# Dealing the maxima of an attention kernel as one stream over all groups, with a lead of three steps

## The chip, the cores and the metric

The kernel runs on one core of one Trainium2 chip. A core has five engines that work beside each other: TensorE (PE in the profile; its weight loads are listed as PEld), VectorE (DVE), ScalarE (ACT), GpSimd (POOL) and SyncE (SP), which here issues DMA transfers. Each engine works through its own queue in the order of the program and waits on semaphores for the others. The metric is the device time of one execution in microseconds (us); less is better.

## The reference

The input x is 4 x 2048 x 256. It is layer-normalised, and the result goes through causal attention with 16 heads of 16 channels with rotary positions, and through a feed-forward network with ternary weights; the output is x plus the attention times the silu of the network.

```python
xn = _layernorm(x)
q, k, v = rope(xn @ Wq.T + bq), rope(xn @ Wk.T + bk), xn @ Wv.T + bv
att = softmax(where(tril, q @ k.T / sqrt(16), -inf))
s = (att @ v) @ Wo.T + bo
g = silu(gelu(xn @ ternary(W1).T + b1) @ ternary(W2).T + b2)
return x + s * g
```

## The kernel before

**Blocks and groups.** The 8192 rows are cut into 16 blocks of 512 rows, four blocks (n = 0, 1, 2, 3) for each batch entry. A block of kind n attends to its own 512 keys and to the n blocks of keys before it, so blocks of kind 0 have the least work and blocks of kind 3 the most. The 16 heads are cut into four groups of four, so the program walks over 64 groups (block, g) in order; below, "group (4,1)" is head group 1 of block 4. Blocks 0, 4, 8 and 12 are of kind 0.

**Two passes for each group.** The softmax takes its maxima first. `maxima(blk, g)` is a Python generator. Each of its steps puts two TensorE products q x k (512 columns each) into two PSUM banks (`s1` in the code, `psum<-kst,qst` in the profile) and has VectorE reduce each of the two to maxima (`mx<-psum`). A group has 8n + 5 steps: 5, 13, 21 or 29. After the last step VectorE reduces the partial maxima (`m<-mx`) and writes them twice into a padded tile (`m_pad<-m`, `m_pad<-m,m_pad`). When the generator is then run to its end, TensorE turns this tile with eight small products (`psum<-id_half,m_pad`, into two banks taken by `two_banks("pt")`) and ScalarE copies the turned maxima to `mT`. I call these eight products the turn. `values(blk, g)` is the second pass. It goes over 4n + 3 units. In a unit TensorE forms scores k x q (`psum<-qst,kst`), adds the turned maxima (`psum<-mT,sel`), ScalarE takes the exponential (`e<-psum`), and TensorE multiplies the exponentials of the unit before by v (`psum<-e,vg`). GpSimd masks the diagonal units. The last products of a group are issued by `end()` after the first unit of the next group; it also copies the sums (`av_sb`) and issues eight small stores of them on SP (`y<-av_sb`, `w<-av_sb`).

**Banks.** PSUM has eight banks. One holds the sums of `values`; the other seven are handed out by `bank` and `two_banks`, which choose by an account (`Course`) that the program keeps while it is written: a cost for each instruction (`work`, line 124, for VectorE, ScalarE and GpSimd) and the time at which each bank should come free. The account chooses banks and nothing else.

**The order around the change.** The main loop (line 1307) runs the units of group i and deals out, between them, the maxima of group i + 1. Each unit has two slots; a slot has a weight, `past` sums the weights passed and `whole` is the sum to be reached. `Paced.to(share)` runs the generator until that share of its work is done. With `whole = sum(slots[:-2]) - END` and END = -100, all steps of group i + 1, with the write to `m_pad`, are out before the last unit's scores. At the end of the group, behind its last unit, `maxs.rest()` (line 1359) issues the turn. So all of the maxima of group i + 1, and no others, lie in group i. Groups of kind 0 have three units. Before the scores of their second unit (u = 1) four steps of the next group are out.

**Loads.** `Loads.go()` is called at the start of each group (line 1311) and when a buffer comes free; it issues on SP the loads of q (`qst<-qd`, 512 KB), of k in chunks (`kst<-kd`, 512 KB each) and of v (`vg<-vd`) up to two groups ahead for q and k. There are three buffers for q, so the q of group i + 2 takes the buffer of group i - 1, which comes free when the last scores of that group have been formed. Since `Loads` goes by head order, the k of group i + 2 follows its q. The same SP queue holds the stores of `av_sb`, the reloads of x (`x_res`), and the reciprocal sums (`rd<-w`, `rw<-rd`).

**Other work in a group.** A projection of a later block (`project`) and a feed-forward pass (`feed`, called gate) are dealt into certain groups; a group with a gate runs it ahead of its units. `further()` pops one step of the output part of the block before (`finish`) at fixed places. In groups (4,2), (8,2) and (12,2) these are `divided` (`yT`) and `projected` (`psum<-yT,woT`), and group g = 3 of these blocks begins with a gate.

Of the kernel before, what the change touches and what calls it, by code (L numbers as in the profile page):

```python
# [37 lines left out]
class Course:  # L38
# [27 lines left out]
    def ready(self, engine, out, ins):  # L66
        t = 0.0
        for ap in ins:
            for k in self.keys(ap):
                if self.by.get(k) != engine:  # L70
                    t = max(t, self.written.get(k, 0.0))
        for k in self.keys(out):
            if self.by.get(k) != engine:
                t = max(t, self.written.get(k, 0.0))
            for other, done in self.read.get(k, {}).items():
                if other != engine:
                    t = max(t, done)
        return t
# [45 lines left out]
    def work(self, engine, op, args):  # L124
        aps = [a for a in args if isinstance(a, bass.AP)]
        out, ins = aps[0], aps[1:]
        n = max(a.free_size() for a in aps)
        if engine == "ACT":
            cost, tail = n / 1.2 + (68 if n > NB else 150), 150
        elif engine == "DVE":  # L130
            cost, tail = n / 0.96 + 67, 135
            if op == "memset":
                cost = n / 0.96 + 60
        else:
            two = op == "tensor_tensor" or op == "scalar_tensor_tensor"
            wide = any(st == 0 and k > 1 for a in ins for st, k in a.ap[1:])
            cost, tail = n * (1.85 if wide else 2.1 if two else 0.9) + 190, 60
        start = max(self.at[engine], self.ready(engine, out, ins))
        self.at[engine] = start + cost
        self.note(engine, out, ins, start + cost + tail)  # L140
# [57 lines left out]
def attention_gated_by_ffn(  # L198
# [38 lines left out]
    FC = FF // P  # L237
    NQ = T // NB
# [205 lines left out]
    def rotation(i, n):  # L444


        wide = pp.tile([P, 2, NB], F32, tag="e", name="wide")[:, 0, :]
        copy = nc.vector.tensor_copy if n == 0 else nc.scalar.copy
        copy(
            wide.rearrange("p (t h f) -> p t h f", t=TT, f=HF),  # L450
            csn[:, i, n * TT : (n + 1) * TT, :].unsqueeze(2).to_broadcast([P, TT, H, HF]),
        )
        yield
        pt = bank("pt")
        for t in range(TT):
            nc.tensor.transpose(
                pt[:, t * P : (t + 1) * P], wide[:, t * P : (t + 1) * P], ident
            )
        if n == 0:
            turn = table0[:, i, :]  # L460
        else:
            turn = pp.tile([P, 2, NB], F32, tag="e", name="turn")[:, 0, :]
        nc.scalar.copy(turn, pt)
        release("pt")
        nc.scalar.dma_start(out=cs[n][i], in_=turn)
# [94 lines left out]
    kst, qst, vst, mTs = {}, {}, {}, {}  # L560
# [12 lines left out]
    def load(blk):  # L573
        xs[blk] = xp.tile([P, TT, D], F32, tag="x", name="xn")
        nc.sync.dma_start(out=xs[blk], in_=x_blk[blk])
# [220 lines left out]
    class Loads:  # L796


        def __init__(self):
            self.free = {"q": 3, "k": 8, "v": 5}  # L800
            self.next = {
                "q": iter(groups),
                "k": iter([(*x, c) for x in groups for c in range(x[0] % NQ + 1)]),
                "v": iter([(*x, c) for x in groups for c in range(x[0] % NQ + 1)]),
            }
            self.head = {k: next(i) for k, i in self.next.items()}
            self.ahead = {"q": 2, "k": 2, "v": 1}
            self.now = 0
# [46 lines left out]
    groups = [(blk, g) for blk in range(NBLK) for g in range(G)]  # L855
    loads = Loads()

    def max_steps(n):


        pairs = range(GH // 2)
        steps = [(c, ((t, j),)) for c in range(n) for t in range(TT) for j in pairs]
        steps += [(n, ((TT - 1, j),)) for j in pairs]
        steps += [(n, ((TT - 2, j), (0, j))) for j in pairs]
        return steps + [(n, tuple((1, j) for j in pairs))]

    def columns(n, c, parts):
        return sum(NB if c < n else (t + 1) * P for t, _ in parts)
# [97 lines left out]
    def value_units(n):  # L966


        pairs, d = range(GH // 2), n * TT
        units = [[((kb, j),) for j in pairs] for kb in range(d + 1)]  # L970
        units.append([((d + 1, j), (d + 3, j)) for j in pairs])
        units.append([tuple((d + 2, j) for j in pairs)])
        return units
# [263 lines left out]
    class Paced:  # L1237
# [6 lines left out]
        def to(self, share):  # L1244
            while self.work and self.done < min(share, 1.0) * self.all - 1e-9:
                next(self.gen, None)
                self.done += self.work.pop(0)
# [3 lines left out]
                pass  # L1251

    K5, PJ, R0 = 6, 8, 19
    CHUNK, BESIDE, SH, END = 200, 300, 0.5, -100
    N_R = 1 + 2 * 2 * (NQ - 1) + 2 * (1 + 12)
    N_Q = TT - 1 + 4 + KC + 4 + TT + 1
    N_T = 2 * 2 * (3 + 2) + N_W - 4
    idle = Paced(iter(()), ())

    def max_work(blk):  # L1260

        n = blk % NQ
        return [columns(n, c, parts) + 80 for c, parts in max_steps(n)]

# [15 lines left out]
    with tc.manual_schedule():  # L1282
        load(0)
        setup()
        rest = Paced(prepare(), [1] * N_R)
        for k, _ in enumerate(project(0)):
            if k == 5 + TT - 1:
                for i in range(2):
                    for _ in rotation(i, 0):
                        pass  # L1290
                rest.to(K5 / N_R)
                gate = feed(0)
                next(gate)
        rest.to(R0 / N_R)
        maxs = Paced(maxima(*groups[0]), max_work(0))
        for k, _ in enumerate(gate):

            rest.to(min(19 + 2 * k + (k > 1), 27 + (k - 4)) / N_R)
            maxs.to((k - 2) / (FC - 2))
            if k == 4:  # L1300
                proj = Paced(project(1), [1] * N_Q)
            if k >= 4:
                proj.to(PJ / N_Q * (k - 3) / (FC - 3))
        maxs.rest()
        rest.rest()
        p0, p1 = 0, 2
        for i, (blk, g) in enumerate(groups):
            n = blk % NQ
            units = len(value_units(n))
            loads.now = i  # L1310
            loads.go()
            nxt = groups[i + 1] if i + 1 < len(groups) else None
            maxs = Paced(maxima(*nxt), max_work(nxt[0])) if nxt else idle
            projs, hids = beside(blk)
            if g in projs:
                proj.rest()
                b2, over = projs[g]
                proj = idle
                if b2 < NBLK:
                    proj, p0, p1 = Paced(project(b2), [1] * (N_Q + N_T)), g, g + over  # L1320

            fast = hids.get(g, NBLK) < NBLK
            slots = [CHUNK] * FC if fast else []
            for u in range(units):
                w = NB if u < units - 1 else NB // 2
                w += 80 + (BESIDE if proj is not idle else 0)
                slots += [w * SH, w * (1 - SH)]
            whole = sum(slots[:-2]) - END
            past = 0
            if fast:  # L1330
                for k, _ in enumerate(gate):
                    past += slots.pop(0) if k < FC else 0

                    if k % 3 == 2:
                        maxs.to(past / whole)
            steps = values(blk, g)
            for u in range(units):
                past += slots.pop(0)
                maxs.to(past / whole)
                next(steps)  # L1340
                if u == units - 2:
                    further()
                past += slots.pop(0)
                maxs.to(past / whole)
                next(steps)
                if u == 0 and ends:
                    ends.pop(0)()
                if u == units // 2 and hids.get(g + 1, NBLK) < NBLK:
                    if b2 == hids[g + 1]:
                        proj.rest()  # L1350
                    gate = feed(hids[g + 1])
                    next(gate)
                if proj is not idle:
                    proj.to(1.05 * (g + (u + 1) / units - p0) / (p1 - p0))
                further()
            for _ in steps:
                pass
            loads.release("q")
            maxs.rest()
            if g == G - 1:  # L1360
                proj.rest()
        for do in ends:
            do()
        for do in deferred:
            if do:
                do()
# [55 lines left out]
```

## Time and profile before

| what | value |
|---|---|
| median of 3 runs (lowest, highest) | 2332.27 us (2331.68, 2336.6) |
| the profiled execution's own time | 2329.72 us |
| its span | 2328.0 us |
| TensorE busy | 2188.2 us (94%), weight loads 1213.3 us (52%) |
| VectorE busy | 1606.3 us (69%) |
| ScalarE busy | 1459.8 us (63%) |
| GpSimd busy | 876.2 us (38%) |
| reductions `mx<-psum` | 2176, mean 683 ns |
| mean granted TensorE clock | 0.985 |

The profiled execution took 2.55 us less than the median of the runs, and its span is 1.72 us shorter than its own time. In the profile's rows "<-" between engines means "waited for". A row of the waits gives the sum of us, the number of waits and the longest. A row of the timeline gives start, length, engine, operation, tiles and in brackets the idle time ahead of it with what ended it. All instructions carry the line of one helper (L161), so rows are told apart by their tiles.

### The profile page before, as it was taken

What the parts mean: (1) busy time and instruction counts of PE and PEld (TensorE: products, weight loads), DVE (VectorE), ACT (ScalarE), POOL (GpSimd) and SP (SyncE); (2) the same over time, 40 slices, a digit from 0 to 9 for tenths busy, and PEclk for the clock granted to TensorE, in tenths of its full rate; (3) what the DMA queues carried; (4) which work ended last, traced back from release to release, by engine and by line L of the source; (5) the groups of instructions that cost most, each with busy time, mean ns of one, the idle gap of its engine ahead of it and who ended that gap; (6) DMA issues with size and microseconds to landing.
All of it is one profiled execution on the core that took longest, in us unless ns stands there. A gap on an engine that the chain in (4) does not pass through costs nothing.

```text
span 2328.0 us, 42716 instructions
## 1 busy us (share of the span) xinstructions
PE 2188.2 (94%) x16596; PEld 1213.3 (52%) x16596; DVE 1606.3 (69%) x2782; ACT 1459.8 (63%) x1697; POOL 876.2 (38%) x1198
## 2 busy tenths in 40 slices
PE   5889999999999999999999999999999999999997
PEld 4555545545455555545545464555555555455553
DVE  8667677776556677687635768768763666777881
ACT  4555656656766565765766565666677556666675
POOL 2137252144534525315344543422534462521000
PEclk8899999999999999999999999999999999999998
DMA  7345344243344525234134443513514353442311
GB/s 228 105 149 172 103 158 128 56 137 108 98 149 128 198 69 166 79 105 156 48 121 142 156 144 102 173 55 102 170 42 158 125 173 101 151 129 55 98 48 34
DMA packets 247611, 280.32 MB, mean 120 GB/s; under 512 B 108784, under 2 KB 143728, under 8 KB 247408
## 3 DMA queue, kind: packets, MB, share of 16 engines
q1 hardware_dynamic: 243680, 271.95, 37.1%
q10 hardware_dynamic: 3728, 5.64, 0.7%
q8 instruction: 131, 2.15, 0.4%
q14 instruction: 72, 0.59, 0.1%
HBM read 181.08 MB, written 87.52 MB: 115 GB/s over the span
## 4 chain that ended last, share of the span: by engine, by line
PE 77%; DVE 12%; ACT 5%; POOL 2%; issue 2%; DMA 1%; ACTq 0%; SPq 0%; DVEq 0%; POOLq 0%
PE psum L161 77%; DVE mx L161 7%; ACT e L161 2%; DVE m_pad L161 1%; ACT L161 1%; DMA kst<-kd 1%; DVE tern L161 1%; POOL xn L161 1%; ACT hh L161 1%; ACT h L161 1%; DVE st L161 0%; POOL xl L161 0%; DVE m L161 0%; POOL xh L161 0%; DVE s L161 0%
## 5 line engine op out<-in xcount | busy, mean ns | idle before, releaser
L161 DVE TENSOR_REDUCE mx<-psum 128x1 f32<-128x512 f32 (+2 forms) x2176 | 1362.2, 683 | 520.0 <-PE psum L161 507.6
L161 ACT ACTIVATE e<-psum 128x1024 f32<-128x1024 f32 x1088 | 1062.5, 1022 | 556.0 <-PE psum L161 547.0
L161 PE MATMUL psum<-kst,qst 64*128 64x512 f32 (+3 forms) x2560 | 561.3, 423 | 36.7 <-ACT e L161 13.6
L161 PE MATMUL psum<-e,vg 128*32 128x512 f32 (+3 forms) x5120 | 577.4, 541 | 0.5 <-POOL e L161 0.5
L161 POOL TENSOR_SCALAR_AFFINE_SELECT e<-e 128x256 f32<-128x256 f32 (+1 forms) x448 | 193.8, 448 | 932.2 <-ACT e L161 924.7
L161 PEld LDWEIGHTS psum<-kst,qst 64*128 64x128 f32 x2560 | 295.0, 186 | 428.6 <-DVE mx L161 243.5
L161 PE MATMUL psum<-qst,kst 64*128 64x512 f32 (+3 forms) x2560 | 478.4, 390 | 20.0 <-DVE mx L161 15.8
L161 PE MATMUL psum<-mT,sel 64*128 64x512 f32 (+3 forms) x2560 | 447.5, 365 | 0.4 <-ACT mT L161 0.4
L161 PEld LDWEIGHTS psum<-qst,kst 64*128 64x128 f32 x2560 | 234.4, 187 | 166.0 <-ACT e L161 65.4
L161 PEld LDWEIGHTS psum<-mT,sel 64*128 64x128 f32 x2560 | 233.8, 187 | 27.8 <-ACT mT L161 1.5
L161 POOL TENSOR_TENSOR hl<-h,hh 128x512 fp32r<-128x512 f32 x128 | 165.2, 1299 | 146.7 <-ACT h L161 114.6
L161 PEld LDWEIGHTS psum<-e,vg 128*32 128x32 f32 x5120 | 112.1, 109 | 135.8 <-issue 115.8
L161 POOL TENSOR_TENSOR r<-qk,cos_sin 128x512 f32<-128x512 f32 x56 | 72.7, 1302 | 192.3 <-DMA cos_sin<-cs 117.8
L161 ACT ACTIVATE hh<-psum,b1c 128x512 fp32r<-128x512 f32 x128 | 88.3, 690 | 87.5 <-PE psum L161 87.2
L161 PE MATMUL psum<-xf,wqkvT 128*128 128x512 f32 x256 | 121.0, 608 | 0.9 <-ACT xf L161 0.9
L161 PE MATMUL psum<-xh,w1T 128*128 128x512 f32 x256 | 105.1, 411 | 3.2 <-DVE s L161 2.7
L161 PE MATMUL psum<-hh,w2T 128*128 128x512 f32 x256 | 107.2, 419 | 0.2 <-ACT w2T L161 0.2
L161 PE MATMUL psum<-xl,w1T 128*128 128x512 f32 x256 | 103.1, 403 | 1.5 <-POOL xl L161 1.5
L161 PE MATMUL psum<-hl,w2T 128*128 128x512 f32 x256 | 102.5, 400 | 0.2
L161 PE MATMUL psum<-mask_k,mask_q 64*128 64x128 bf16 (+1 forms) x1280 | 99.3, 213 | 0.0
L161 ACT ACTIVATE qk<-psum,bqk 128x512 f32<-128x512 f32 x64 | 44.1, 689 | 85.8 <-PE psum L161 85.8
L161 ACT ACTIVATE h<-psum,b1c 128x512 f32<-128x512 f32 x128 | 87.8, 686 | 0.0
(125 smaller groups left out, 1551.5 us busy)
## 6 DMA issues: line engine op xcount, KB each, us to landing
kst<-kd SPq DMA_DIRECT2D x160, 512.0 KB
qst<-qd SPq DMA_DIRECT2D x64, 512.0 KB
vg<-vd SPq DMA_DIRECT2D x160, 166.0 KB
qd<-qkhi SPq DMA_DIRECT2D x32, 512.0 KB
qd<-qklo SPq DMA_DIRECT2D x32, 512.0 KB
kd<-qkhi SPq DMA_DIRECT2D x30, 512.0 KB
kd<-qklo SPq DMA_DIRECT2D x30, 512.0 KB
vd<-v SPq DMA_DIRECT2D x16, 574.0 KB
```

Of the source, the lines that this page charges most:

```text
L161: made = call(*args, **kwargs)
```

## The change

The maxima are dealt out by one object, `Ahead`, that lives over all groups. It counts steps, not columns. In group i it is led to `ends[i + 1] + LEAD` with LEAD = 3, `ends` being the running sum of the groups' steps; so when group i ends, the maxima of group i + 1 are all out and three steps of group i + 2 as well. A step is taken only if the program has already issued the loads of the q and k chunk that it reads (`ready`). `whole` is now the sum of all slots, the last unit's too. The turn of group i + 1 is issued by `turn` ahead of the scores of group i's last unit, and not behind them. In a group of kind 0 the counts after its six slots become 1, 2, 3, 4, 5 and 5 (of 5): the first two are the last two steps of group i + 1, and the third, ahead of the scores of unit u = 1, is the first step of group i + 2. In the account, a VectorE step costs at least 205 ns.

```diff
-            cost, tail = n / 0.96 + 67, 135
+            cost, tail = max(n / 0.96 + 67, 205), 135
...
-    CHUNK, BESIDE, SH, END = 200, 300, 0.5, -100
+    CHUNK, BESIDE, SH, LEAD = 200, 300, 0.5, 3
...
+    class Ahead:
+        def __init__(self):
+            self.i, self.done, self.left, self.gen = -1, 0, 0, None
+            self.ends, self.turns = [], {}
+            for blk, _ in groups:
+                self.ends.append((self.ends or [0])[-1] + len(max_steps(blk % NQ)))
+        def ready(self):
+            if self.left:
+                blk, g = groups[self.i]
+                c = max_steps(blk % NQ)[-self.left][0]
+            elif self.i + 1 < len(groups):
+                (blk, g), c = groups[self.i + 1], 0
+            else:
+                return False
+            return (blk, g) in qst and (blk, g, c) in kst
+        def to(self, count):
+            while self.done < count - 1e-9 and self.ready():
+                if not self.left:
+                    self.i += 1
+                    self.left = len(max_steps(groups[self.i][0] % NQ))
+                    self.gen = maxima(*groups[self.i])
+                next(self.gen)
+                self.left -= 1
+                self.done += 1
+                if not self.left:
+                    self.turns[self.i] = self.gen
+        def turn(self, i):
+            if i < len(groups):
+                for _ in self.turns.pop(i):
+                    pass
...
-        maxs = Paced(maxima(*groups[0]), max_work(0))
+        maxs = Ahead()
...
-            maxs.to((k - 2) / (FC - 2))
+            maxs.to(min((k - 2) / (FC - 2), 1) * maxs.ends[0])
...
-        maxs.rest()
+        maxs.to(maxs.ends[0])
+        maxs.turn(0)
...
-            nxt = groups[i + 1] if i + 1 < len(groups) else None
-            maxs = Paced(maxima(*nxt), max_work(nxt[0])) if nxt else idle
+            due = maxs.ends[min(i + 1, len(groups) - 1)] + LEAD
+            begun = maxs.done
...
-            whole = sum(slots[:-2]) - END
+            whole = sum(slots)
...
             for u in range(units):
                 past += slots.pop(0)
-                maxs.to(past / whole)
+                maxs.to(begun + past / whole * (due - begun))
+                if len(slots) == 1:
+                    maxs.turn(i + 1)
                 next(steps)
...
             loads.release("q")
-            maxs.rest()
```

More of the change, by code (lines that the diff above doesn't have):

```diff
@@ L1258, in attention_gated_by_ffn @@
     idle = Paced(iter(()), ())
-    def max_work(blk):
-        n = blk % NQ
-        return [columns(n, c, parts) + 80 for c, parts in max_steps(n)]
+    class Ahead:
[28 more added lines that the diff above has]
+                    pass
     def beside(blk):
@@ L1338, in attention_gated_by_ffn @@
                 past += slots.pop(0)
-                maxs.to(past / whole)
+                maxs.to(begun + past / whole * (due - begun))
+                if len(slots) == 1:
+                    maxs.turn(i + 1)
                 next(steps)
@@ L1343, in attention_gated_by_ffn @@
                 past += slots.pop(0)
-                maxs.to(past / whole)
+                maxs.to(begun + past / whole * (due - begun))
+                if len(slots) == 1:
+                    maxs.turn(i + 1)
                 next(steps)
```

## The prediction

> **What bounds the kernel now.** I read the page first: the engines' shares and the chain that ended last.
>
> ```profile
> PE 2188.2 (94%) x16596; PEld 1213.3 (52%) x16596; DVE 1606.3 (69%) x2782; ACT 1459.8 (63%) x1697; POOL 876.2 (38%) x1198
> PE 77%; DVE 12%; ACT 5%; POOL 2%; issue 2%; DMA 1%; ACTq 0%; SPq 0%; DVEq 0%; POOLq 0%
> ```
>
> TensorE is busy for 2188.2 of 2328.0 us, so all of its idle time is 139.8 us, the start and the tail included. A change in the order of VectorE's work can only win from that. The second view is the waits of TensorE (sum, number, longest).
>
> ```profile
> PE psum L161 <- DVE m_pad L161: 34.8, 46, 1.6
> PE psum L161 <- DVE mx L161: 22.8, 51, 3.8
> PEld psum L161 <- ACT mT L161: 14.6, 38, 0.7
> PE psum L161 <- DMA kst<-kd: 2.5, 3, 1.1
> ```
>
> The largest wait is that of the turn for `m_pad`: 46 of the 64 group ends, 0.76 us each. The timeline of one such end, group (6,3) to (7,0), shows its shape, VectorE first and then TensorE:
>
> ```profile
> 1013.09 1.29 DVE L161 TENSOR_REDUCE mx<-psum 128x2 f32<-128x512 f32 x2 [0.20 <-PE psum L161]
> 1014.41 0.25 DVE L161 TENSOR_REDUCE m<-mx 128x16 f32<-128x96 f32 x1
> 1014.70 0.28 DVE L161 CAST m_pad<-m 128x16 fp32r<-128x16 f32 x1
> 1015.01 0.18 DVE L161 TENSOR_TENSOR m_pad<-m,m_pad 128x16 fp32r<-128x16 f32 x1
> ```
>
> ```profile
> 1014.32 0.40 PE L161 MATMUL psum<-mT,sel 64*128 64x256 f32 x4
> 1015.33 0.43 PE L161 MATMUL psum<-id_half,m_pad 64*68 64x64 f32 x8 [0.62 <-DVE m_pad L161]
> ```
>
> The last reductions, m and the two writes take 2.1 us on VectorE (1013.09 to 1015.19); TensorE has only the last unit's scores and one product with v to lay over them, and then stands still. Afterwards VectorE is empty and waits for the first step of the next group.
>
> The third view is the short groups of kind 0, where loads are late already. SP and TensorE, group (4,1), which starts at 670.89:
>
> ```profile
> 672.34 0.43 SPq L161 DMA_DIRECT2D x_res<-in_L_attn_x_dram  x1
> 672.82 0.50 SPq L161 DMA_DIRECT2D vg<-vd  x1
> 673.42 0.44 SPq L161 DMA_DIRECT2D qst<-qd  x1
> 673.91 0.47 SPq L161 DMA_DIRECT2D kst<-kd  x1
> ```
>
> ```profile
> 675.66 0.50 PE L161 MATMUL psum<-kst,qst 64*128 64x384 f32 x4
> 681.61 0.50 PE L161 MATMUL psum<-kst,qst 64*128 64x512 f32 x2 [0.97 <-DMA kst<-kd]
> ```
>
> The k for group (4,3) is issued at 673.91 and lets TensorE go at 681.61, 7.7 us later. It is used just after group (4,1) has ended, and even so TensorE waits 0.97 us. The row at 675.66 is the step ahead of the scores of unit u = 1.
>
> **Part 1: the turn's wait goes.** In a group of 29 steps the last one for group i + 1 is dealt at 26/29 = 0.90 of the slots, and three further steps lie between it and the turn: six reductions, 6 x 0.683 = 4.1 us of VectorE work behind `m_pad`. When TensorE issues the turn, most of these have been fed, so `m_pad` is done. The wait is removed whole: 34.8 us less the part in blocks of kind 0, which I count in part 3 (waits by window: 1.4 us in each of blocks 4, 8 and 12 and 1.5 us in block 0, in all 5.7): 29.1 us.
>
> What is late next? Behind the turn, TensorE waits again for a bank (0.26 us on `mx` at 1017.43, the same 0.26 at 2232.68), since VectorE begins from nothing. If all 46 ends had it, that is 12 us, and if the steady stream has it too, 0. I take 5. Against it, the turn takes two banks and ScalarE's copy to `mT` (580 ns) in the midst of a unit, while up to three steps hold six of the seven banks. The nearest row is the wait of weight loads for `mT`, 14.6 us over 38 times, which is there already and merely moves; at worst it doubles and all of it shows. So the part is worth between 29.1 - 14.6 = 14.5 and 29.1 + 12 = 41 us; I take 29.1 + 5 = 34. VectorE's total is unchanged: the number of steps is the same, and only their places differ.
>
> **Part 2: the floor in the account.** It touches no instruction, only which bank is chosen. The steps concerned (`m` 203 to 253 ns, `m_pad` 328 and 293 ns, `bn_aggr` 182 ns) come nearer to their measured lengths. Bank waits of TensorE (22.8 on `mx`, 13.6 on `e`) bound what choices can do, in either direction; few choices lie just behind these steps. I take 0, with 5 us to each side.
>
> **Part 3: the lead meets loads that are not there.** In groups of 13 to 29 steps the first step of group i + 2 comes at 0.77 of the group or later, over 10 us after the loads were issued (the shortest is group (5,2): issued at 792.8, due at 788.3 + 0.77 x 20.0 = 803.7): hidden. A group of kind 0 has five steps, and the step ahead of the scores of u = 1 reads q and k of group i + 2, issued at the start of the same group; `ready` does not stop it, since in program order the load has been issued. TensorE stands there, and behind it on its queue the scores of u = 1, hence ScalarE's exponentials and everything after.
>
> Landing: from the first issue at 672.34 to 681.61, x_res, v, q and k (512 + 166 + 512 + 512 = 1702 KB) take 9.27 us, 184 KB/us. I use that rate for the others.
> - (4,0): v store, v, q and k (574 + 166 + 512 + 512 KB) from 659.53: k of (4,2) lands at about 669.1. The step was at 666.35; with one step fewer ahead of it (0.5) and a bank wait gone (0.2), TensorE arrives at 665.7 and waits 3.4 us. The turn's 0.69 and the 0.2 are saved: the group ends 2.5 us late.
> - (4,1): arrives at 675.66 + 2.5 - 0.9 = 677.3. The loads on SP stand behind the `av_sb` stores, issued ahead of the first stall, so they come no later; k lands at about 681. Wait 3.7. With 0.69 and 0.97 saved the group's successor starts 3.5 us late.
> - (4,2): its loads follow `rw<-rd` at 683.76 (256 + 166 + 512 + 512 KB, 7.9 us: 691.7), some 1.4 us later by the delay of `av_sb`: 693.1. TensorE arrives at 686.13 + 3.5 - 0.9 = 688.7 and waits 4.4. Behind it lie 8.4 us of work up to the gate of (4,3) (686.13 to 694.64, less 0.15 of a wait for `yT`). It starts at 701.5 and not at 694.64: 6.8 us lost.
>
> The gate of (4,3) is fed by GpSimd's splits, which come after the exponential and mask of u = 1, so they are delayed alike. Block 8 is like block 4 (6.8). In block 12 no store of v stands ahead: q and k from 1786.98 land 5.6 us later, about when TensorE arrives; with the first wait gone I take 5. In block 0 the k of (1,0) is issued at 127.12, behind four stores of k; by the two rates of landing (5.6 us for q and k from 125.82, or 7.7 from 127.12) it is there at 131.4 to 134.8, say 132.5. The step was at 125.96; the 5.7 us from it to the gate at 131.66 hold 1.5 us of wait for `m_pad`. The gate starts at 132.5 + 4.2 = 136.7: 5 us lost. In all 2 x 6.8 + 5 + 5 = 23.6 us, between 14 (each landing 2 us sooner) and 32 (each 2 us later).
>
> [...]
>
> **The sum.** 34 saved, 23.6 lost: 10 us less. The profiled execution's own 2329.72 becomes 2320; against the median of the runs, 2332.27, it is 2322.
>
> **The rivals.**
> - No new wait for loads (chance 0.22): the k lands earlier because less is queued ahead of it than the rate says; part 1 stands alone, 34 less: 2298. For it speaks that the first such load (661.91) is read at 671.13 with no wait; against it the 7.7 us row.
> - Slower by the loads (0.20): in the three groups of a kind-0 block the waits add up in full (3.4 + 3.7 + 4.4 = 11.5, three blocks, and 5 in block 0: 40) because what I count as saved (bank waits, the turn's waits) is spent on other waits. The point is 34 / 4 = 8.5 us for each block: above it the change loses. 40 - 34 = 6 more: 2338.
> - The turn's wait only changes its name (0.16): the turn in the midst of a unit waits for two banks, at half of the 14.6, with no refill gain: 29.1 - 7.3 - 23.6 = 2 more: 2334.
>
> **How the numbers follow.** My forecast, waits gone at the long groups and loads late at the short ones, has 0.42. What a measurement of this kernel can tell from no change is about 0.2%, 4.7 us. Faster: 0.36 of the forecast's 0.42, all 0.22 of the first rival and 0.02 of the third: 0.60. Same: 0.06 + 0.03 (second) + 0.08 (third): 0.17. Slower: 0.17 + 0.06: 0.23. The range runs from 2298, the first rival's middle (11 in 100 below it), to 2341, the second rival's 2338 with 3 us of the unknown landing: 19 in 100 are left out. The forecast's own range is 2307 to 2332.
>
> **What would show it.** Right: the wait of `psum` for `m_pad` nearly gone; a wait for `kst<-kd` of some 35 to 45 us in about ten places, all in the first three groups of blocks 4, 8 and 12 and in (0,2); long groups 0.6 to 0.9 us shorter. Wrong: no kst wait above 5 us in all (first rival), waits for `mx` or `e` ahead of the turn or the last scores of 10 us or more (third), or blocks 4, 8 and 12 over 8.5 us longer in their first three groups (second).

## The result and the profile after

The changed kernel takes 2340.8 us (median of 18 runs, 2336.05 to 2342.48) against 2331.8 us before (18 runs): a ratio of 1.0035 with a 95% interval of 1.0026 to 1.0043. It is slower, by little but clear of the noise, and stands at the top of my stated range (2298 to 2341). The profiled execution has a span of 2339.3 us, 11.3 more than before.

The page of the changed kernel first, engines and chain:

```profile
PE 2188.5 (94%) x16596; PEld 1219.1 (52%) x16596; DVE 1606.2 (69%) x2782; ACT 1457.9 (62%) x1697; POOL 875.4 (37%) x1198
PE 76%; DVE 8%; ACT 7%; DMA 4%; issue 3%; POOL 2%; SPq 1%; ACTq 0%; POOLq 0%; DVEq 0%
```

TensorE's busy time is the same to 0.3 us, so all 11 us are idle time. In the chain VectorE has gone from 12% to 8%, and DMA from 1% to 4%. The waits of TensorE, changed kernel, say the same (sum, number, longest):

```profile
PE psum L161 <- DMA kst<-kd: 39.3, 10, 8.7
PE psum L161 <- ACT e L161: 21.7, 40, 0.9
PE psum L161 <- DVE mx L161: 16.2, 39, 0.9
...
PE psum L161 <- POOL e L161: 6.4, 5, 1.5
```

The row for `m_pad`, 34.8 us before, is gone; that for `kst<-kd` has grown from 2.5 to 39.3 us, and `e` (13.6 before) and the mask of GpSimd (0.5) took back 14 us.

The end of group (6,3) in the changed kernel, VectorE and then TensorE:

```profile
1016.20 0.25 DVE L161 TENSOR_REDUCE m<-mx 128x16 f32<-128x96 f32 x1
1016.48 0.18 DVE L161 CAST m_pad<-m 128x16 fp32r<-128x16 f32 x1
1016.69 0.18 DVE L161 TENSOR_TENSOR m_pad<-m,m_pad 128x16 fp32r<-128x16 f32 x1
1016.79 2.47 DVE L161 TENSOR_REDUCE mx<-psum 128x1 f32<-128x512 f32 x4
```

```profile
1018.95 0.50 PE L161 MATMUL psum<-kst,qst 64*128 64x512 f32 x2
1019.28 0.38 PE L161 MATMUL psum<-id_half,m_pad 64*68 64x64 f32 x8
1019.49 0.48 PE L161 MATMUL psum<-qst,kst 64*128 64x256 f32 x4
```

`m_pad` is written 2.4 us before the turn reads it, VectorE goes straight on, and none of these rows has a bracket. That is the gain. The loss is in the short groups. The chain of waits of the changed kernel between 661 and 704 us, groups (4,0) to (4,2) (start, length, what; with pieces left out):

```profile
660.81 6.10 DMA kst<-kd
...
671.77 6.09 DMA kst<-kd
...
685.19 7.03 DMA kst<-kd
...
694.84 1.83 POOL e L161 x4
...
700.10 1.27 POOL xl L161
...
701.40 0.76 DVE s L161
...
702.20 2.09 PE psum L161 x3
```

Three loads of k stand in the chain for 19.2 of 43 us, one behind the other. From the third the chain runs over the exponential, GpSimd's mask, its splits for the gate, VectorE's `s`, and only then TensorE.

To see where the time lies I compare the starts of the copies of `av_sb`, one for each group, in both traces. From the copy of the last group before block 4 to that of group (4,3): 65.3 us before, 75.6 after, so 10.3 lost; block 8 10.4, block 12 14.4, block 0 6.0: 41.2 us lost in the blocks of kind 0. The groups of kinds 1, 2 and 3 (the "long groups" below) have gained 9.2, 7.9 and 11.5: 28.6 us. The rest, 1.3 us, is gained at the start and in the tail. 41.2 - 28.6 - 1.3 are the 11.3 us of the span.

### The profile page after: what moved, and what is told of

The parts are those of the page before. It is cut to its first block, busy times and chain, and to the rows that moved or that the text cites. A ratio compares the mean times of both kernels' runs of the same rounds, so it can differ in the third digit from the quotient of the medians.

```text
span 2339.3 us, 42621 instructions
## 1 busy us (share of the span) xinstructions
PE 2188.5 (94%) x16596; PEld 1219.1 (52%) x16596; DVE 1606.2 (69%) x2782; ACT 1457.9 (62%) x1697; POOL 875.4 (37%) x1198
## 4 chain that ended last, share of the span: by engine, by line
PE 76%; DVE 8%; ACT 7%; DMA 4%; issue 3%; POOL 2%; SPq 1%; ACTq 0%; POOLq 0%; DVEq 0%
PE psum L161 76%; DVE mx L161 5%; ACT e L161 3%; DMA kst<-kd 2%; ACT L161 1%; ACT hh L161 1%; SPq L161 1%; ACT h L161 1%; ACT g L161 1%; POOL e L161 1%; DVE m_pad L161 0%; ACT mT L161 0%; POOL xl L161 0%; DMA vg<-vd 0%; DMA rd<-w 0%
## 5 line engine op out<-in xcount | busy, mean ns | idle before, releaser
L161 PE MATMUL psum<-kst,qst 64*128 64x512 f32 (+3 forms) x2560 | 575.4, 425 | 71.9 <-DMA kst<-kd 39.3
L161 PE MATMUL psum<-qst,kst 64*128 64x512 f32 (+3 forms) x2560 | 491.9, 389 | 19.6 <-DVE mx L161 9.9
L161 PE MATMUL psum<-mT,sel 64*128 64x512 f32 (+3 forms) x2560 | 459.2, 368 | 0.0
L161 PEld LDWEIGHTS psum<-qst,kst 64*128 64x128 f32 x2560 | 246.6, 189 | 116.7 <-ACT e L161 51.8
L161 PEld LDWEIGHTS psum<-mT,sel 64*128 64x128 f32 x2560 | 242.1, 189 | 25.3 <-ACT mT L161 0.2
L161 ACT CAST mT<-psum 68x512 fp32r<-68x512 f32 x64 | 37.2, 581 | 99.1 <-PE psum L161 99.1
```

What stands on the lines that cost most here:

```text
L161: made = call(*args, **kwargs)
```

## The experiments

Each is given as its difference from the changed kernel, unless it says from before; ratios are to the kernel before, run on the same chip. "Short groups" below is the sum over the blocks of kind 0, against before, by the same copies of `av_sb`; like every sum of waits it is read from one profiled execution of each run.

**1. No lead in the short groups.**

```diff
-            due = maxs.ends[min(i + 1, len(groups) - 1)] + LEAD
+            lead = 0 if n == 0 and g < G - 1 else LEAD
+            due = maxs.ends[min(i + 1, len(groups) - 1)] + lead
...
-                if len(slots) == 1:
+                if len(slots) == 1 and lead:
...
+            if not lead:
+                maxs.turn(i + 1)
```

> The changed kernel, but in the first three groups of the blocks of kind 0 (0, 4, 8, 12) the lead is 0 and the turn stands behind the last unit as before; everywhere else lead 3 and the early turn. Theory (the loss is loads asked for too early in the short groups, the gain of the long groups is real): the waits of TensorE for kst fall from 39.3 us to under 4 us, the wait for m_pad stays under 8 us, and the time is about 28 us under the kernel before: 2300 to 2308. Rival 1 (the early turn, which takes two banks in the midst of a unit, or the steady stream costs in the long groups): no faster than before, 2328 to 2345. Rival 2 (the account's floor has re-dealt the banks for the worse): 2315 to 2335, since only a part is removed.

Measured: 0.997 (0.9958 to 0.9982), 2325.75 us. Faster than before, but not by 28 us: the wait for `kst` is down to 2.2 us, yet TensorE waits 15.3 us for `m_pad` in 7 places; without lead and with the new pace a short group's last step comes only in its last unit. Short groups: 18.9 us lost. My number was wrong by 18 us, in the main for a part I had left in, which experiment 5 takes out. The time lies in the range of rival 2 (the floor), which this run does not exclude; experiments 3 and 6 do.

**2. The turn behind the last unit, lead 3.**

```diff
-                if len(slots) == 1:
-                    maxs.turn(i + 1)
...
             loads.release("q")
+            maxs.turn(i + 1)
```

> The changed kernel with lead 3 everywhere, but the turn stands behind the last unit as before. Theory: the same as the changed kernel within 6 us (2335 to 2346), since the lead alone has m_pad ready and the loads are as late as before; the wait for kst stays at 35 to 43 us. Rival 1 (the early turn costs): 10 us or more faster than the changed kernel, under 2331.

Measured: 1.0053 (1.0038 to 1.0069), 2344.27 us, within the theory's range and not separable from the changed kernel. The place of the turn trades: the long groups gain 19.4 us in place of 28.6, the short ones lose 32.0 in place of 41.2. In the sum, then, the early turn is not what costs.

**3. Without the floor in the account.**

```diff
-            cost, tail = max(n / 0.96 + 67, 205), 135
+            cost, tail = n / 0.96 + 67, 135
```

> The changed kernel without the floor of 205 ns in the account. Theory: the same as the changed kernel within 5 us (2336 to 2346). Rival 2 (the floor chooses worse banks): 8 us or more faster, under 2333. The wait for kst 35 to 43 us either way.

Measured: 1.012 (1.0104 to 1.0136), 2361.79 us: 20 us slower than the changed kernel. Neither theory had this: the floor helps, and by much. The loss against the changed kernel is 13.5 us in blocks of kind 2 and 5.1 in kind 3; in all the long groups gain 10.9 us in place of 28.6. The timeline shows one such place, group (1,3) to (2,0), without the floor, VectorE and TensorE:

```profile
326.95 0.24 DVE L161 TENSOR_REDUCE m<-mx 128x16 f32<-128x80 f32 x1
327.22 1.27 DVE L161 CAST m_pad<-m 128x16 fp32r<-128x16 f32 x1
...
328.62 1.53 DVE L161 TENSOR_TENSOR yT<-y,rw 128x512 f32<-128x512 f32 x1
330.08 1.28 DVE L161 TENSOR_REDUCE mx<-psum 128x1 f32<-128x512 f32 x2
```

```profile
330.81 0.79 PE L161 MATMUL psum<-kst,qst 64*128 64x512 f32 x1 [2.42 <-DVE mx L161]
```

A lead step was given the bank of the reduction at 330.08, which stood behind `m`, `m_pad` and `yT`. With the floor in the account the same step was given another bank:

```profile
325.51 0.50 PE L161 MATMUL psum<-kst,qst 64*128 64x512 f32 x1 [0.33 <-ACT e L161]
```

**4. Lead 1.**

```diff
-    CHUNK, BESIDE, SH, LEAD = 200, 300, 0.5, 3
+    CHUNK, BESIDE, SH, LEAD = 200, 300, 0.5, 1
```

> The changed kernel with lead 1 in place of 3. In a short group the first step of group i + 2 then comes about one unit (4 us) later, and the turn follows the last maxima step after one further step only. Theory: kst waits fall to 3 to 15 us, but the turn waits for m_pad again, some 0.5 to 1 us at each of 60 ends (30 to 60 us): 2325 to 2345 in all. If the lead were not what makes m_pad ready, the wait for m_pad would stay near 0 and the time would be under 2315.

Measured: 1.0061 (1.0045 to 1.0077), 2345.11 us. It is at the upper end of what I expected: `kst` falls to 15.4 us, `m_pad` is back at 47.6 us in 45 places, and the long groups gain 0.4 us in place of 28.6. So the lead makes `m_pad` ready, and the same lead makes the loads late.

**5. Short groups as before.** Experiment 1 with the old pace in the short groups:

```diff
-            whole = sum(slots)
+            whole = sum(slots) if lead else sum(slots[:-2]) + 100
...
-                maxs.to(begun + past / whole * (due - begun))
+                maxs.to(begun + min(past / whole, 1) * (due - begun))
```

> As the run without lead in the short groups, but these groups also keep the pace of before (all steps out ahead of the last unit, the turn behind it). In the run before, their last step came only in the last unit and the turn waited 15.3 us for m_pad. Theory: that wait falls under 8 us, the short groups cost as in the kernel before within 8 us, the long groups keep their gain of about 26 us: 2302 to 2315. Rival (short groups lose by the order of the stream itself and not by loads and m_pad): 2320 or more.

Measured: 0.992 (0.9905 to 0.9935), 2312.83 us: within the theory's range. The wait for `m_pad` falls to 3.9 us. Short groups lose 8.9 us, just over the 8 I allowed, with 7.0 us of `kst` left; the long ones gain 25.8.

**6. The floor alone, in the kernel before.**

```diff
-            cost, tail = n / 0.96 + 67, 135
+            cost, tail = max(n / 0.96 + 67, 205), 135
```

> The kernel before with nothing but the floor of 205 ns in the account. Without it the changed kernel lost 21 us. If the floor is worth that by itself: 2308 to 2316. Theory now: it mends choices of banks at places that only the stream makes tight, so alone it is worth little: within 6 us of the kernel before, 2326 to 2338.

Measured: 0.9982 (0.9973 to 0.9991), 2327.03 us. By itself it gains 4 us; under the stream it is worth 20.

**7. Loads a group earlier.**

```diff
-    kp = ctx.enter_context(tc.tile_pool(name="kp", bufs=8))
+    kp = ctx.enter_context(tc.tile_pool(name="kp", bufs=7))
...
-    qp = ctx.enter_context(tc.tile_pool(name="qp", bufs=3))
+    qp = ctx.enter_context(tc.tile_pool(name="qp", bufs=4))
...
-            self.free = {"q": 3, "k": 8, "v": 5}
+            self.free = {"q": 4, "k": 7, "v": 5}
...
-            self.ahead = {"q": 2, "k": 2, "v": 1}
+            self.ahead = {"q": 3, "k": 3, "v": 1}
```

> The changed kernel with a fourth buffer for q and the loads of q and k up to three groups ahead in place of two; to make room, seven buffers for k in place of eight. Order of the maxima as in the changed kernel. Theory (loads asked for too early): the wait for kst falls from 39.3 us to under 8 us, the short groups lose under 10 us against the kernel before in place of 41, and the time is 2300 to 2316. Rival (the order of the stream in the short groups costs by itself): short groups still lose 25 us or more, 2325 or more.

Measured: 0.9917 (0.9902 to 0.9932), 2311.39 us. The same order of maxima, and 1.2% (27 us) less than the changed kernel. Waits of TensorE in this run:

```profile
PE psum L161 <- DVE yT L161: 22.4, 11, 9.2
...
PE psum L161 <- DMA kst<-kd: 6.5, 1, 6.5
```

One wait for `kst` is left, in block 0. The long groups gain 28.5 us; the short groups lose 11.8, a little more than the 10 I had, now in part to `yT`. This part is the price of the earlier loads and not of the stream: experiment 9 has these loads without the stream, its short groups lose 10.8 us, and its wait for `yT` is 18.1 us in place of 10.2 before.

**8. TensorE kept busy while it waits.** Idle products ahead of the waiting step:

```diff
+            self.now = -1
...
                 if not self.left:
+                    blk, g = groups[max(self.now, 0)]
+                    if blk % NQ == 0 and g < G - 1 and 0 <= self.now == self.i - 1:
+                        for k in range((3, 3, 5)[g]):
+                            s1 = bank("s1")
+                            nc.tensor.matmul(s1, ident, wqkvT[:, 0, :NB], start=True, stop=True)
+                            release("s1")
                     self.i += 1
...
             loads.go()
+            maxs.now = i
```

> The changed kernel with idle products put ahead of the step that waits for k: three, three and five products of 128 x 512 float32 columns (about 0.96 us each) in the first, second and third group of each block of kind 0, into a bank that nobody reads. This adds 44 products. If TensorE's half-speed windows come from standing still, the windows in blocks 4, 8 and 12 (10, 14 and 20 us of them in the changed kernel) shrink to under 5 us each, and the time falls or stays in spite of the added work: 2326 to 2341. If they come from something else, they stay, and the time rises by what the fill exceeds the waits: 2343 to 2355.

Measured: 1.0056 (1.0039 to 1.0072), 2344.16 us. I asked this because in the changed kernel TensorE runs at about half speed after several of the waits (granted clock 0.53 from 679.4 to 682.8 us, for one). Stretches 658 to 730, 1218 to 1297 and 1786 to 1866 us (length, busy time of the engines, granted clock, DMA), changed kernel and then with the fill:

```profile
658.00:730.00 72.00, 58.24 (x506) 36.73 (x504) 35.97 (x64) 39.32 (x49) 26.93 (x40) 0.93 0.38 115
...
1786.00:1866.00 80.00, 63.81 (x527) 40.27 (x528) 36.40 (x64) 41.35 (x51) 27.63 (x42) 0.87 0.33 103
```

```profile
658.00:730.00 72.00, 64.88 (x502) 38.59 (x502) 35.03 (x62) 39.41 (x50) 27.54 (x41) 0.98 0.38 115
...
1786.00:1866.00 80.00, 73.33 (x554) 43.16 (x554) 36.87 (x64) 43.62 (x54) 27.50 (x41) 0.96 0.35 108
```

Three of the idle products take 2.84 us, 0.95 each. The fill lifts the clock from 0.93 to 0.98 and from 0.87 to 0.96 and covers all but 9.2 us of `kst`, and still the short groups lose 42.2 us. Neither branch of my expectation came whole: the windows shrink, from 10, 14 and 21 us to some 3, 6 and 6 (worked out from the clock of the three stretches), and the time does not fall. So in these two runs the half clock shrank with the standing still, but lifting it won nothing here: TensorE comes to the second product with Wo earlier and waits there for `s`, 3.8 us in each of blocks 4, 8 and 12 in place of 2.2 to 2.4.

**9. The earlier loads alone, in the kernel before** (the edit of 7 without the stream).

> The kernel before with the earlier loads alone (four buffers for q, seven for k, three groups ahead), no stream. The control for the changed kernel with earlier loads, which was 0.9917 of before. Theory (loads cost only where the stream asks for them early; before waits 2.5 us for kst in all): within 7 us of the kernel before, 2325 to 2337. If the earlier loads are worth 20 us by themselves, the reading of that run falls: under 2316.

Measured: 1.0033 (1.002 to 1.0045), 2340.08 us: a little slower than before, and just outside my range. So the loads (with one k buffer less) gain nothing without the stream, and experiment 7's 0.9917 belongs to the two together.

**10. A fifth buffer for `s`.**

```diff
-    kp = ctx.enter_context(tc.tile_pool(name="kp", bufs=8))
+    kp = ctx.enter_context(tc.tile_pool(name="kp", bufs=7))
...
-    tp = ctx.enter_context(tc.tile_pool(name="tp", bufs=4))
+    tp = ctx.enter_context(tc.tile_pool(name="tp", bufs=5))
...
-            self.free = {"q": 3, "k": 8, "v": 5}
+            self.free = {"q": 3, "k": 7, "v": 5}
```

> The changed kernel with a fifth buffer for the tiles that xf, xh, xl, yT and s share, so that s need not wait until GpSimd has read xf; seven buffers for k make room. Loads and stream as in the changed kernel. Theory (in the third short group the late k also holds up GpSimd's splits, these hold s, and the second product with Wo waits for s, 2.3 us in each of blocks 4, 8 and 12): the wait for s falls from 7.6 to under 3 us, the third short groups shorten by 2 to 3 us each, kst stays at 35 to 43 us: 2329 to 2337. If that wait merely hides another, the time stays within 3 us of the changed kernel, 2338 to 2344.

Measured: 1.0024 (1.0015 to 1.0033), 2336.92 us: in the theory's range, but over all runs only some 2.6 us better than the changed kernel's 1.0035, with intervals that overlap. The wait for `s` falls from 7.6 to 0.7 us, and the stretch from the third wait for `kst` to the gate takes 9.7, 10.1 and 9.1 us in blocks 4, 8 and 12 in place of 11.9, 11.6 and 12.0. The chain by `s` is real, at 6.6 us in the profile. The short groups lose 34.1 in place of 41.2, but these 7 us are not that chain alone: block 12 wins 5.7, blocks 4 and 8 only 1.2 and 0.4, since their third wait for `kst` grows from 4.6 and 4.1 to 7.3 and 8.3 us. In all `kst` stands at 45.5, above the 35 to 43 I expected.

**11. Experiments 5 and 7 together.**

> The short groups dealt as in the kernel before (no lead, old pace, late turn), the long ones as in the changed kernel, and the earlier loads. Theory: the long groups' 26 us stay, and the short groups' 9 us that were left without lead fall by the 7.0 us of kst still waited for there: 2300 to 2310. If the two mends do the same work, no better than each alone: 2310 to 2316.

Measured: 0.9918 (0.9904 to 0.9931), 2312.59 us: no better than each alone. The `kst` wait is gone, waits for `yT` (22.2 us) stand in its place, and the short groups lose 16.1 us.

**12. Only k earlier.**

```diff
-            self.ahead = {"q": 2, "k": 2, "v": 1}
+            self.ahead = {"q": 2, "k": 3, "v": 1}
```

> The changed kernel with only the loads of k up to three groups ahead; buffers as they were, so q still waits for the buffer of group i - 1. Theory: the step now waits for q in place of k; q stands first of the two, and the 512 KB of k no longer share its way, so the wait is shorter by 1 to 3 us at each of ten places: waits for qst and kst together 12 to 30 us, 2318 to 2334. If the landing time is fixed and not a matter of what is queued, the waits stay at 35 us or more: 2337 or more.

Measured: 1.0013 (1.0004 to 1.0022), 2334.82 us, just above my range. Waits of TensorE in this run:

```profile
PE psum L161 <- issue: 19.3, 6, 4.2
...
PE psum L161 <- DMA qst<-qd: 13.9, 4, 9.8
```

TensorE waits for q in place of k in 4 places. The 6 waits under "issue", for which the profile shows no releaser, stand before the same steps, in the second and third groups of blocks 4, 8 and 12. Together they are 33.2 us in the ten places where k had 39.3: above the 12 to 30 I expected, just below the 35 of the other branch. By 184 KB/us, 512 KB less ahead of the step is 2.8 us at each place; it was 0.6. So this run does not show that what is queued ahead sets the landing, and what does stays open. The wait for `s` is 11.9 us, and the short groups still lose 32.4.

## Why the prediction was wrong

I forecast 10 us less and it is 9 more. The two mechanisms, the turn's wait going and the loads coming late, were right; what the late loads cost was wrong, and with it the direction. Between the forecast (34 saved, 23.6 lost) and the profile (11.3 more) lie 21.7 us: 17.6 too little in part 3, 5.4 too much in parts 1 and 2, less the 1.3 won at the start.

**Part 1, the turn's wait: it went, but not by the stream alone.** I had 34 us; the long groups gained 28.6. `m_pad`'s 34.8 us went whole, and the weight loads' wait for `mT`, which I feared would double, fell from 14.6 to 6.7 us. `e` and the mask took 14 us, and `mx` returned 6.6, where I had counted 5. Experiment 4 shows that it is the lead that does it. But the gain needs the floor as well: without it (experiment 3) the long groups gain 10.9 us, less than the 14.5 that I had as the lower end of this part.

**Part 2, the floor: the price was wrong.** I took 0 with 5 us to each side, because "few choices lie just behind these steps". Alone it is worth 4 us (experiment 6), but under the stream 20 (experiment 3): at the place shown there, a lead step follows directly behind m and `m_pad`. That the other places are like it I have not shown. The two parts of the change are not a sum. Without the floor the stream costs 28 us. I should have costed the floor on the order after, not on the trace of before.

**Part 3, late loads: the waits right, what they cost wrong.** I said 35 to 45 us of `kst` in about ten places: 39.3 in 10. In block 4 I had waits of 3.4, 3.7 and 4.4; they were 2.75, 2.81 and 4.62. But I turned 11.5 us of wait into 6.8 of loss, and block 4 lost 10.3; 41.2 us in all and not 23.6. The step that failed is "Behind it lie 8.4 us of work up to the gate of (4,3)". The gate's first product before, and then the third wait, the wait for `s` and the gate in the changed kernel:

```profile
694.64 0.51 PE L161 MATMUL psum<-xh,w1T 128*128 128x512 f32 x1
```

```profile
692.31 0.50 PE L161 MATMUL psum<-kst,qst 64*128 64x512 f32 x2 [4.62 <-DMA kst<-kd]
...
702.20 2.94 PE L161 MATMUL psum<-yT,woT 128*128 128x512 f32 x4 [2.35 <-DVE s L161]
704.16 1.42 PE L161 MATMUL psum<-xh,w1T 128*128 128x512 f32 x1
```

From the third wait's end (692.31) to the gate (704.16) it took 11.9 us: the late scores delayed GpSimd's mask and splits, these delayed `s`, and the second product with Wo waited 2.35 us for `s`. I had written that the splits are "delayed alike" and let TensorE's own work lie over them. Two experiments bear this out. Without the wait for `s` (experiment 10) the stretch is 9.7 us. With the fill (experiment 8) a row of four score products behind the third step takes 0.45 us, where the changed kernel has 0.80 at half clock (0.54 from 693.1 to 696.5), and the stretch still takes 12.3 us (12.5 and 12.6 in blocks 8 and 12): the half clock ahead of the wait for `s` is not what lengthens it.

The rest is smaller. Counted from the copy of `av_sb` ahead of block 4, the third step came 8.3 us later than before, and my sum had 7.0: of the 10.2 us waited, 1.9 were saved elsewhere, and I had counted on 4.5. Behind the gate 1.3 us came back. That block 4 lost just what its three waits amount to is the outcome of these terms and not a rule.

In block 12 I took 5 us and it was 14.4. The first wait, 2.77 us, is followed by half speed (granted clock 0.52 from 1799 to 1805.8), and the copy of `av_sb` behind it comes 4.6 us later in the block than before; in block 4, at full clock there (1.00 from 667.1 to 675.3), it comes 1.6 us later. Its stores stand on SP ahead of the third load, which comes 4.7 us later, and the third wait is 8.7 us. One stall makes a later load late, which my sum for block 12 left out.

The rival "slower by the loads" was the one whose numbers came: its 40 us of loss (measured 41.2), and 2338, with the point at 8.5 us for each block; measured 10.3, 10.4 and 14.4. I gave it 0.20. Of its mechanism, savings spent on other waits, the runs show the wait for `s`, 7.6 us where it was 3.4. The rival without a wait for loads is excluded by the 39.3 us. Against that of the renamed wait stand the long groups' 28.6 us, where it had 22, and the turn itself, whose products have no idle time before them any more.

The three loads of k in the chain of block 4, 512 KB each, took 6.1, 6.1 and 7.0 us from issue to landing in the changed kernel, with loads of v and q issued up to 2.2 us ahead of each on SP. The forecast went by 184 KB/us, from the row in which TensorE went on 7.7 us after the issue.

What stays open: how block 12's 14.4 us divide between the half clock and the late third load (the fill of experiment 8 brought them to 11.9, and blocks 4 and 8 to 11.8 and 11.6), and why the third waits for `kst` grew in experiment 10, which also has one k buffer less.

## What to carry to other kernels

A lead in the order of one stage is a demand on the loads of that stage: find the shortest group, and ask there whether the load has landed when the lead asks, not on the average group. Here the long groups gained 29 us and the short ones lost 41; leaving the short groups as they were (0.992), or issuing the loads one group earlier with the stream (0.9917), beats both kernels. And where a wait on one engine also holds up others, the work behind it does not shrink to that engine's own: follow each of the others to the place where they meet again. Here TensorE had 8.4 us of work to the gate, and the way over GpSimd's splits and `s` took 11.9.

## What the runs showed of the hardware

In this trace TensorE's granted clock falls to about half (0.52 to 0.54 over stretches of 3.4 to 6.8 us) after some short waits and stays at 1.00 after others. In the changed kernel, block 4 (start and end, length, busy times, granted clock, DMA share, GB/s):

```profile
674.60:678.00 3.40, 0.59 (x17) 0.14 (x6) 1.59 (x5) 0.65 (x2) 0.41 (x1) 1.00 0.76 280
...
679.40:682.80 3.40, 3.40 (x24) 1.39 (x22) 1.76 (x3) 1.84 (x2) 1.53 (x4) 0.53 0.14 30
...
699.80:702.20 2.40, 0.05 (x2) 0.00 (x0) 0.80 (x2) 2.36 (x3) 2.07 (x3) 1.00 0.55 137
703.30:706.70 3.40, 3.40 (x8) 2.04 (x7) 0.79 (x2) 0.00 (x0) 0.00 (x0) 0.53 0.68 254
```

A wait of 2.81 us, ended at 678.0, and one of 2.35 us, ended at 702.2, are each followed by a stretch of 3.4 us at about half speed, 1.4 and 1.1 us later. The wait of 2.75 us that ended at 667.0 in the same block is not (granted clock 1.00 from 667.1 to 670.5), while that of 2.77 us in block 12 is followed by 6.8 us of it (0.52 from 1799 to 1805.8). So in this case the length of a wait does not tell by itself. In experiment 8 the fill removed some two thirds of the half-speed time in the three stretches (mean granted clock 0.93, 0.91 and 0.87 in the changed kernel, 0.98, 0.96 and 0.96 with the fill), and the time did not fall: TensorE only waited longer for `s`, 12.0 us in place of 7.6.
